# Graph attention on one core: 17 instead of 16 of 52 score pairs weighted by GpSimd, and loads of q and k that write one copy each

## The chip, the core and the metric

The kernel runs on one core of a Trainium2 chip. A core has a matrix engine (TensorE, PE in the profile; its weight loads are PEld), a vector engine (VectorE, DVE), an engine for functions such as the exponential (ScalarE, ACT), an engine of general processors (GpSimd, POOL), and a sequencer that here only issues transfers (SyncE, SP). Each takes its instructions in order and waits for the others by semaphores. Transfers run on 16 DMA engines that all queues share. SBUF is the memory on the chip, PSUM the one that TensorE writes its results into, and DRAM is outside. The metric is device time in microseconds (us); less is better.

## The reference, cut to what matters

```python
def _L1_gnn_ref(x, spatial_encoding, edge_encoding, Wq, Wk, Wv, Wo):
    n, d = x.shape                      # 3327, 128
    h = Wq.shape[0] // d                # 8
    scale = d ** (-0.5)
    q = (x @ Wq.T).reshape(d, n, h)
    k = (x @ Wk.T).reshape(d, n, h)
    v = (x @ Wv.T).reshape(d, n, h)
    a = jnp.einsum('dnh,dmh->dnm', q, k) * scale
    a = a + spatial_encoding + edge_encoding
    a = jax.nn.softmax(a, axis=2)
    out = jnp.einsum('dnm,dmh->dnh', a, v)
    out = out.reshape(n, h * d)
    return out @ Wo.T

# --- layer 0 ---
h = jnp.maximum(_layernorm(x, axis=-1), 0.0)
x = x + _L0_gnn_ref(h, adj, ...)        # one product with adj.T, a batch norm, relu
# --- layer 1 ---
h = jnp.maximum(_layernorm(x, axis=-1), 0.0)
x = x + _L1_gnn_ref(h, adj, adj, ...)
```

All values are fp32. Layer 1 is nearly the whole time. It has 128 batches ("d"), each an attention of 3327 queries over 3327 keys with only 8 numbers per query, and the same 3327 x 3327 matrix, twice adj, is added to the scores of every batch. So the exponentials, 128 x 3327 x 3327 of them, and the sums with the matrix weigh as much as the matrix products.

## The kernel before, in words

**Cutting.** Layer 1 takes the batches in 32 groups of G = 4. Within a group the queries come in 7 blocks (`qblocks`: six of 480, one of 448), the keys in NC = 26 chunks of 128 (key m is in chunk m mod 26). Scores lie with the keys on partitions and the queries along the free dimension. For one chunk and one block, the four batches make two *pairs* (`half` 0 and 1), so a block has 52 pairs. `SU = 13` steps of four pairs make a block; 91 steps make a group; the program is written out flat, with no loop on the chip.

**A pair's way.** `product` makes the scores of both batches into one PSUM tile `s` (two banks, three such tiles). q and k are held as two parts each (a rounded value and its remainder[...]), so each batch takes 32 rows: q's rows are (part 0, part 0, part 1, part 1), 8 rows each, k's rows are (part 0, part 1, part 0, part 1), and their product over 32 rows is the full one. This is why every load of q and k writes its source twice.

There are then two ways. A **plain** pair: VectorE adds the matrix (tile `at`, loaded from `in_adjT`) to the scores and writes `d`; ScalarE later takes the exponential of all plain pairs of the step in one instruction (`late`, L970). A **weighted** pair: ScalarE takes the exponential of the bare scores from PSUM (`f`, L934), and GpSimd multiplies it with the exponential of the matrix (tile `wt`, L937), which was computed once and kept in DRAM as `wd`. Either way `second` multiplies the result with v on TensorE three steps later (`LAG = 3`, L670), into one of two PSUM banks `av`.

**Which pair goes which way.** `kinds` gives every step its pairs. Chunks 0 to WC - 1 are plain, WC = 18 to 25 weighted: 36 and 16 pairs. A step has three plain pairs and one weighted, and the steps in `DOUBLE = (3, 7, 11)` have two and two. So ScalarE's order in a step is f, then the d of the step before; in a double step a second f follows.

**Tiles and loads.** `fetch(x + PRE)` issues on SP what the step two ahead needs first: `at` tiles of two chunks (480 KB, four buffers, 9 a block), `wt` tiles of one chunk (240 KB, three buffers, 8 a block). A load waits on SP until its buffer is free (VectorE's last use for at, GpSimd's for wt), and all that SP issues after it waits too.

**Beside the steps.** During a group, `loads` brings q, k and v of the next one: k in two halves through a staging tile `ks`, sorted by casts on GpSimd (L194), q directly, v in three loads. These items, 33 per group, are spread evenly over steps 4 to 87 (in group 0: over steps 39 to 87, `FROM`). `projections` computes q, k and v of the next but one group in blocks 0 to 2 (k in 0, q in 1, v in 2; in group 0 of two groups): `begin` puts its product into the other av bank in a double step (7 or 11), `go_on` empties it in the same step on VectorE, two more instructions on GpSimd round it (L240, L241), and in the next step (8 or 12) SP stores it (L247 for q and k, L222 for v). In groups 30 and 31 there is none. `outputs` does the last product with Wo in blocks 3 and 4. `finish` divides a finished block of av: three pieces at the steps in `PARTS = (3, 7, 8)`; L702 and L704 store.

**The first group.** `wd` doesn't exist yet. For block 0 `weigh_early` makes it at the end of layer 0; for each later block, `more_weights` does so during the block before: in a cycle of three steps two chunks of the matrix are loaded (L814), two steps later ScalarE takes their exponential (L819), and at the next cycle SP stores them (L806). Before the first step, `first_loads` brings k (all chunks, 4 loads, L879), q of block 0 (8 loads, L883), v (L885); the rest of q (`others`, 8 loads, L915) follows two a step from step 2 on.

The loads of q and k in the code:

```python
qs = qT[:, bass.ds(d * N + n0, n)].rearrange("(a h) n -> a h n", h=H)
...
    q[p0 + a * 2 * H : p0 + (a + 1) * 2 * H, n0 : n0 + n].bitcast(F32),
    qs[a].unsqueeze(0).to_broadcast([2, H, n]),
...
ks = kT[:, bass.ds(d * N + n0, n)]
...
    k[p0 : p0 + 4 * H].bitcast(F32), ks.unsqueeze(0).to_broadcast([2, 2 * H, n])
```

Of the kernel before, what the change touches and what calls it, by code (L numbers as in the profile page):

```python
# [9 lines left out]
F32 = mybir.dt.float32  # L10
# [8 lines left out]
N = 3327  # L19
D = 128  # L20
H = 8
P = 128
NC = 26
T = N * D
NP = NC * P
NB = 512
QB = 480
# [2 lines left out]
HALF = 0.5 / math.sqrt(D)  # L30
SAFE = 30.0
SU = NC // 2
WC = 18
CH = 4 * NP // D
NG = D // G
DOUBLE = (3, 7, 11)
PARTS = (3, 7, 8)

# [6 lines left out]
def tile_two_layer_gnn(  # L47
# [34 lines left out]
    kT = dram.tile([2 * H, TP], F32, name="kT")  # L82
# [6 lines left out]
    wd = dram.tile([NC - WC, P, NP], F32, name="wd")  # L89
# [4 lines left out]
    adjr = adjT.rearrange("(p c) n -> p c n", c=NC)  # L94
# [43 lines left out]
    def q_loads(q, p0, d, n0=0, n=NP):  # L138

        qs = qT[:, bass.ds(d * N + n0, n)].rearrange("(a h) n -> a h n", h=H)  # L140
        return [
            (
                q[p0 + a * 2 * H : p0 + (a + 1) * 2 * H, n0 : n0 + n].bitcast(F32),
                qs[a].unsqueeze(0).to_broadcast([2, H, n]),
            )
            for a in range(2)
        ]

    def k_loads(k, p0, d, n0, n):
        ks = kT[:, bass.ds(d * N + n0, n)]  # L150
        return [(
            k[p0 : p0 + 4 * H].bitcast(F32), ks.unsqueeze(0).to_broadcast([2, 2 * H, n])
        )]

    def v_loads(v, d):
        W = NC * (H + 1)
# [152 lines left out]
    with tc.tile_pool(name="l0", bufs=1) as l0, tc.tile_pool(  # L309
        name="l0adj", bufs=3  # L310
    ) as ap, tc.tile_pool(name="l0s", bufs=4) as sp, tc.tile_pool(
        name="l0last", bufs=1
# [13 lines left out]
        cols = l0.tile([P, 4], F32, name="cols")  # L326
# [162 lines left out]
        for c in range(NC):  # L489
            a = tiles[c]  # L490
# [37 lines left out]
            i = c - 2 * NQ - 5  # L528
# [3 lines left out]
        weights = []  # L532
        for n0 in range(0, NB, NB // 2):
            a = ap.tile([P, 7 * NB], F32, name="a")
            a8 = a[:, : 8 * (NB // 2)].rearrange("p (c n) -> p c n", c=8)
            nc.sync.dma_start(a8, adjr[:, WC:, n0 : n0 + NB // 2])
            weights.append((a8, n0, NB // 2))

# [18 lines left out]
        for i, (n0, w) in enumerate(blocks):  # L557
            s = slice(n0, n0 + w)
# [150 lines left out]
    def attention():  # L709
# [3 lines left out]
        with tc.tile_pool(name="exd", bufs=4) as ep, tc.tile_pool(  # L713
            name="adj", bufs=4
        ) as ap, tc.tile_pool(name="adw", bufs=3) as wp, tc.tile_pool(
            name="exf", bufs=6
        ) as fp, tc.tile_pool(name="res", bufs=2) as rp, tc.tile_pool(
            name="wk", bufs=2
        ) as wk, tc.tile_pool(name="psc", bufs=3, space=PSUM) as psc, tc.tile_pool(
            name="pav", bufs=1, space=PSUM  # L720
# [6 lines left out]
            if True:  # L727
# [14 lines left out]
                for s in range(SU):  # L742
                    j, k = (sum(len(x[i]) for x in kinds) for i in range(2))
                    n = 2 if s in DOUBLE else 1
                    kinds.append((
                        [(x // 2, x % 2) for x in range(j, j + 4 - n)],
                        [(WC + x // 2, 1 - x % 2) for x in range(k, k + n)],
                    ))


                wanted, have = [], {}
                for x, (i, y, s) in enumerate(steps):
                    n0, w = qblocks[y]
# [9 lines left out]
                def fetch(x):  # L763
                    while wanted and wanted[0][0] <= x:
                        _, kind, i, y, c = wanted.pop(0)
                        n0, w = qblocks[y]
                        if kind:
                            a = wp.tile([P, QB], F32, name="wt")
                            nc.sync.dma_start(a[:, :w], wd[c - WC, :, n0 : n0 + w])
                        else:  # L770
                            a = ap.tile([P, 2, QB], F32, name="at")
                            n = min(2, WC - 2 * c)
                            nc.sync.dma_start(
                                a[:, :n, :w], adjr[:, 2 * c : 2 * c + n, n0 : n0 + w]
                            )
                        have[kind, i, y, c] = a
# [20 lines left out]

                def more_weights(i, y, s):

                    k, phase = divmod(s, 3)  # L800
                    if i or y + 1 >= len(qblocks):
                        return
                    n0, w = qblocks[y + 1]
                    c = WC + 2 * k
                    if phase == 0 and k:
                        nc.sync.dma_start(  # L806
                            wd[c - 2 - WC : c - WC, :, n0 : n0 + w].rearrange("c p n -> p c n"),
                            have["w"][:, :, :w],
                        )
                    if c == NC:  # L810
                        return
                    if phase == 0:
                        have["w"] = wk.tile([P, 2, QB], F32, name="t4")
                        nc.sync.dma_start(  # L814
                            have["w"][:, :, :w], adjr[:, c : c + 2, n0 : n0 + w]
                        )
                    elif phase == 2:
                        a = have["w"][:, :, :w]
                        nc.scalar.activation(a, a, AF.Exp, bias=low, scale=2.0)  # L819
# [3 lines left out]
                extra, begun = [], []  # L823

                def begin(i, y, s):
                    if extra and s in DOUBLE[1:]:
                        begun.append(extra.pop(0))
                        drive(begun[0], avs2[(i * len(qblocks) + y + 1) % 2])

# [72 lines left out]
                for x, (i, y, s) in enumerate(steps):  # L902
                    n0, w = qblocks[y]
                    fetch(x + PRE)
                    k = x - i * SU * len(qblocks) - FROM[i]
                    if k == 0 and i + 1 < NG:
                        pending = loads(sets[(i + 1) % 2], at(i + 1))
                        total = len(pending)

                    while pending and (total - len(pending)) * (SU * len(qblocks) - FROM[i] - 4) <= k * total:  # L910
                        pending.pop(0)()
                    more_weights(i, y, s)
                    if x > 1:
                        for args in others[:2]:
                            nc.sync.dma_start(*args)  # L915
                        del others[:2]
                    due = len(waiting) == LAG
                    plain, rest = pairs(s)
                    d = ep.tile([P, 3, 2, QB], F32, name="d")
                    es = [d[:, j] for j in range(len(plain))]  # L920

                    def add(j, p):
                        c = plain[j][0]

                        nc.vector.scalar_tensor_tensor(  # L925
                            d[:, j, :, :w],
                            have[0, i, y, c // 2][:, c % 2, :w]
                            .unsqueeze(1).to_broadcast([P, 2, w]),
                            SAFE / 2, p[:, :, :w], ALU.min, ALU.add,
                        )  # L930

                    def weighted(c, p):
                        f = fp.tile([P, 2, QB], F32, name="f")
                        nc.scalar.activation(  # L934
                            f[:, :, :w], p[:, :, :w], AF.Exp, scale=2.0
                        )
                        nc.gpsimd.tensor_tensor(  # L937
                            f[:, :, :w], f[:, :, :w],
                            have[1, i, y, c][:, :w].unsqueeze(1).to_broadcast([P, 2, w]),
                            ALU.mult,  # L940
                        )
                        es.append(f)

                    if coming is None:
                        coming = first(x)
                    weighted(rest[0][0], coming)
                    coming = None
                    if late is not None:
                        late()
                    add(0, product(i, y, *plain[0]))  # L950
                    second(0)
                    if s == DOUBLE[1]:
                        step()
                    add(1, product(i, y, *plain[1]))
                    if len(rest) > 1:
                        weighted(rest[1][0], product(i, y, *rest[1]))
                    else:
                        add(2, product(i, y, *plain[2]))
                    if s in PARTS and s != DOUBLE[1]:
                        step()  # L960

                    if s - 1 in DOUBLE and x + 1 < len(steps):
                        coming = first(x + 1)
                    second(1)
                    begin(i, y, s)
                    go_on(i, y, s)

                    def late(d=d, w=w, n=len(plain)):
                        flat = d[:, :n].rearrange("p j x n -> p (j x) n")[:, :, :w]
                        nc.scalar.activation(flat, flat, AF.Exp, scale=2.0)  # L970

                    waiting.append(((i, y, s), es))
# [207 lines left out]
```

## Time and profile before

| | |
|---|---|
| time, median of 3 runs | 10234.54 us (10231.9 to 10239.35) |
| the profiled execution | 10253.06 us, its span 10251.3 us |
| granted clock of TensorE, mean | 0.981 |
| TensorE busy | 95% of the span |
| VectorE busy | 91% |
| ScalarE busy | 96% |
| GpSimd busy | 82% |
| DMA | 1735.75 MB, mean 169 GB/s |
| loads of q for a next group (L172) | 248, 208 KB each |
| loads of ks for a next group (L172) | 248, 208 KB each |
| products with the weights on GpSimd (L937) | 3584, mean 2233 ns |

The profile is of one execution. A group of instructions is written as line, engine, operation, output<-inputs with partitions x elements, count, then busy time in us and the mean in ns of one, then the idle time of the engine just before them and what ended most of it. A timeline row is the start, the time taken, engine, line, operation, and in brackets the idle time before it with what ended it; x2 behind a row merges two neighbours. A row of waits is who waited for whom, us in total, times, the longest. "SPq" is SyncE's queue. A matmul's end is modelled, so a busy TensorE isn't TensorE at its peak.

### The profile page before, as it was taken

Reading aid. Unit: us, or ns where it says so; the run is one execution under the profiler, and the core shown is the slowest. Engines: PE = TensorE matmul, PEld = TensorE weight load, DVE = VectorE, ACT = ScalarE, POOL = GpSimd, SP = SyncE. Lnnn points to the kernel's source line nnn. Section 1 sums busy time; section 2 is a strip of 40 time slices with the busy share of each in tenths; the row PEclk is TensorE's granted clock in tenths of the full one; section 3 lists DMA queues with packets and bytes.
Section 4 is the critical chain, followed back from the end, with each engine's and each line's share of the span. In section 5 each row is a group of like instructions: output and inputs, shape, how many; then the busy total and the mean of one; then the engine's idle time right before and its main releaser. Section 6 shows DMA issues by size and latency. Waiting matters only on the chain.

```text
span 10251.3 us, 186610 instructions
## 1 busy us (share of the span) xinstructions
PE 9787.2 (95%) x71535; PEld 2720.9 (27%) x71535; DVE 9306.6 (91%) x9527; ACT 9886.6 (96%) x6662; POOL 8434.3 (82%) x4325
## 2 busy tenths in 40 slices
PE   7899999999999999999999999999999999999998
PEld 3122222222222222222222222222222222222222
DVE  5689999999999999999999999999999999999998
ACT  4799999999999999999999999999999999999998
POOL 1678888888888888888888888888888888888887
PEclk8899999999999999999999999999999999999999
DMA  6665666655666555666556665555666555656554
GB/s 238 195 188 162 169 173 169 170 164 164 169 173 170 168 165 165 170 171 168 168 161 167 168 174 168 164 168 163 170 169 170 167 163 168 171 167 170 162 158 129
DMA packets 1035806, 1735.75 MB, mean 169 GB/s; under 512 B 116086, under 2 KB 1011828, under 8 KB 1027092
## 3 DMA queue, kind: packets, MB, share of 16 engines
q1 hardware_dynamic: 1032399, 1718.85, 59.4%
q8 instruction: 561, 9.19, 0.4%
q0 software_dynamic: 784, 4.03, 0.1%
q14 instruction: 346, 2.83, 0.1%
q10 hardware_dynamic: 1716, 0.85, 0.0%
HBM read 1621.03 MB, written 102.37 MB: 168 GB/s over the span
## 4 chain that ended last, share of the span: by engine, by line
POOL 30%; PE 25%; ACT 20%; issue 11%; DMA 11%; DVE 2%; SPq 1%; POOLq 0%; ACTq 0%; DVEq 0%
POOL f L937 29%; PE av L670 13%; ACT f L934 11%; PE s L785 9%; ACT d L970 9%; DMA at<-in_adjT 6%; DMA wt<-wd 2%; DVE d L925 2%; PE acc L502 1%; DMA t<-in_adjT 1%; PE av L210 1%; POOL k L194 1%; DMA q<-qT 1%; POOL o L241 1%; POOL o L240 0%
## 5 line engine op out<-in xcount | busy, mean ns | idle before, releaser
L925 DVE SCALAR_TENSOR_TENSOR d<-at,s 128x960 f32<-128x960 f32 x8064 | 8733.3, 1138 | 632.9 <-PE s L785 361.2
L937 POOL TENSOR_TENSOR f<-f,wt 128x960 f32<-128x960 f32 (+1 forms) x3584 | 7933.3, 2233 | 1552.2 <-ACT f L934 1322.0
L970 ACT ACTIVATE d<-d 128x2880 f32<-128x2880 f32 (+1 forms) x2912 | 7071.3, 2428 | 97.0 <-DVE d L925 95.8
L670 PE MATMUL av<-d,v 128*9 128x480 f32 x32256 | 5126.0, 573 | 0.6 <-ACT d L970 0.6
L785 PE MATMUL s<-q,k 32*128 32x480 f32 x23296 | 4267.6, 479 | 412.8 <-ACT f L934 179.9
L934 ACT ACTIVATE f<-s 128x960 f32<-128x960 f32 (+1 forms) x3584 | 3443.7, 987 | 54.7 <-PE s L785 48.4
L785 PEld LDWEIGHTS s<-q,k 32*128 32x128 f32 x23296 | 1801.2, 183 | 5745.0 <-DVE d L925 3710.2
L670 PE MATMUL av<-f,v 128*9 128x480 f32 x14336 | 2876.7, 570 | 0.0
L670 PEld LDWEIGHTS av<-d,v 128*9 128x9 f32 x32256 | 585.1, 88 | 1228.0 <-issue 1226.1
L670 PEld LDWEIGHTS av<-f,v 128*9 128x9 f32 x14336 | 317.8, 88 | 154.0 <-issue 139.3
L194 POOL CAST k<-ks 128x256 fp32r<-128x256 f32 x434 | 284.2, 655 | 0.0
L241 POOL TENSOR_TENSOR o<-pf,o 104x512 fp32r<-104x512 f32 x124 | 159.5, 1287 | 9.9
L502 PE MATMUL acc<-a,A 128*128 128x512 f32 (+1 forms) x364 | 152.1, 570 | 9.2 <-DMA a<-in_adj 9.1
L680 DVE STREAM_TRANSPOSE avs<-av 128x480 f32<-128x480 f32 (+1 forms) x224 | 149.5, 667 | 4.4 <-PE av L670 4.4
L512 DVE TENSOR_REDUCE amax<-a 128x1 f32<-128x3327 f32 x26 | 93.7, 3604 | 27.8 <-DMA a<-in_adj 27.8
L444 POOL TENSOR_SCALAR o<-ident,rdeg 128x128 f32<-128x128 f32 x26 | 15.2, 601 | 110.1 <-DVE rdeg L441 110.1
L502 PEld LDWEIGHTS acc<-a,A 128*128 128x128 f32 x364 | 68.9, 192 | 94.9 <-issue 93.4
L509 ACT ACTIVATE junk<-a 128x3327 bf16<-128x3327 f32 x26 | 77.3, 2974 | 6.5 <-DMA a<-in_adj 6.5
L239 DVE TENSOR_SCALAR pf<-av,low_half 104x512 f32<-104x512 f32 x62 | 46.5, 751 | 40.0 <-PE av L210 38.8
L237 DVE COPY pf<-av 104x512 f32<-104x512 f32 x62 | 42.8, 691 | 39.5 <-PE av L210 39.5
L819 ACT ACTIVATE t<-t,low_half 128x960 f32<-128x960 f32 (+1 forms) x24 | 26.2, 1090 | 52.2 <-DMA t<-in_adjT 49.2
L240 POOL CAST o<-pf 104x512 fp32r<-104x512 f32 x124 | 76.1, 613 | 0.0
(131 smaller groups left out, 916.7 us busy)
## 6 DMA issues: line engine op xcount, KB each, us to landing
at<-in_adjT SPq DMA_DIRECT2D x1728, 480.0 KB
wt<-wd SPq DMA_DIRECT2D x1536, 240.0 KB
at<-in_adjT SPq DMA_DIRECT2D x288, 448.0 KB
wt<-wd SPq DMA_DIRECT2D x256, 224.0 KB
ks<-kT SPq DMA_DIRECT2D x248, 208.0 KB
q<-qT SPq DMA_DIRECT2D x248, 208.0 KB
a<-in_adj SPq DMA_DIRECT2D x26, 1663.5 KB
kT<-o SPq DMA_DIRECT2D x128, 208.0 KB
```

Source lines behind the costliest of these rows:

```text
L194: nc.gpsimd.tensor_copy(k[:, c : c + n, half * 64 : half * 64 + 64], ks.bitcast(F32).rearrange("g (p c) -> g c p", c=NC)[:, c : c + n, :],)
L210: nc.tensor.matmul(bank[:CH], hj, wqk[s][:, e * NB : (e + 1) * NB], start=True, stop=True)
L241: nc.gpsimd.tensor_tensor(o[:CH, 1], f[:CH], of[:CH, 0], ALU.subtract)
L502: nc.tensor.matmul(acc[i][:, :w], A[:, c, :], a[:, n0 : n0 + w], start=(c == 0), stop=(c == NC - 1),)
L512: nc.vector.tensor_reduce(amax[:, c : c + 1], a[:, :N], AX.X, ALU.max, apply_absolute_value=True)
L670: nc.tensor.matmul(av[32 * b : 32 * b + H + 1, :w], tiles[2][:, b, c, :], e, start=first, stop=last,)
L680: nc.vector.transpose(avs[:, :J, :].rearrange("p j h -> p (j h)"), av[:, : 32 * J].rearrange("p (q j) -> p j q", j=J),)
L785: nc.tensor.matmul(p[:, x, :we], k[rs, c, :], q[rs, n0 : n0 + we], start=True, stop=True,)
L925: nc.vector.scalar_tensor_tensor(d[:, j, :, :w], have[0, i, y, c // 2][:, c % 2, :w] .unsqueeze(1).to_broadcast([P, 2, w]), SAFE / 2, p[:, ...
L934: nc.scalar.activation(f[:, :, :w], p[:, :, :w], AF.Exp, scale=2.0)
L937: nc.gpsimd.tensor_tensor(f[:, :, :w], f[:, :, :w], have[1, i, y, c][:, :w].unsqueeze(1).to_broadcast([P, 2, w]), ALU.mult,)
L970: nc.scalar.activation(flat, flat, AF.Exp, scale=2.0)
```

## The change

Five things change together.

- One pair more goes the weighted way: 35 plain pairs (`PP`), 17 weighted. Chunk 17 (`WC` is now 17) has its half 0 plain and its half 1 weighted, so it is loaded both as part of an `at` tile and as a `wt` tile (9 a block), and `wd` has nine chunks.
- Four double steps instead of three: 2, 5, 8 and 11. A block has 9 steps of 3 + 1 and 4 of 2 + 2.
- What hangs on those steps moves: the pieces of `finish` to steps 5, 8 and 9, the begin of a side product to 8 and 11 (its store to 9 and 12). The weighted pairs take their halves in the order 0, 1 instead of 1, 0.
- `more_weights` takes three chunks in a cycle of four steps instead of two in three (loads at steps 0, 4, 8, exponentials at 2, 6, 10, stores at 4, 8, 12); `weigh_early` nine chunks instead of eight.
- Each load of q and k writes one copy: for q four loads of 8 rows per batch instead of two with a broadcast source, for k two of 16 rows instead of one. A group's k and q take 32 loads instead of 16, its list 49 items instead of 33; `first_loads` has 8 and 16 of them instead of 4 and 8, `others` 16 instead of 8. The bytes are the same.

```diff
-WC = 18
+PP = 35
+WC = PP // 2
 CH = 4 * NP // D
 NG = D // G
-DOUBLE = (3, 7, 11)
-PARTS = (3, 7, 8)
+DOUBLE = (2, 5, 8, 11)
+PARTS = (5, 8, 9)
...
         qs = qT[:, bass.ds(d * N + n0, n)].rearrange("(a h) n -> a h n", h=H)
         return [
-            (
-                q[p0 + a * 2 * H : p0 + (a + 1) * 2 * H, n0 : n0 + n].bitcast(F32),
-                qs[a].unsqueeze(0).to_broadcast([2, H, n]),
-            )
-            for a in range(2)
+            (q[p0 + i * H : p0 + (i + 1) * H, n0 : n0 + n].bitcast(F32), qs[i // 2])
+            for i in range(4)
         ]
 
     def k_loads(k, p0, d, n0, n):
-        ks = kT[:, bass.ds(d * N + n0, n)]
-        return [(
-            k[p0 : p0 + 4 * H].bitcast(F32), ks.unsqueeze(0).to_broadcast([2, 2 * H, n])
-        )]
+        cols = bass.ds(d * N + n0, n)
+        return [
+            (k[p0 + i * 2 * H : p0 + (i + 1) * 2 * H].bitcast(F32), kT[:, cols])
+            for i in range(2)
+        ]
...
-            a8 = a[:, : 8 * (NB // 2)].rearrange("p (c n) -> p c n", c=8)
+            a8 = a[:, : (NC - WC) * (NB // 2)].rearrange("p (c n) -> p c n", c=NC - WC)
...
-                        [(WC + x // 2, 1 - x % 2) for x in range(k, k + n)],
+                        [((PP + x) // 2, (PP + x) % 2) for x in range(k, k + n)],
...
-                            n = min(2, WC - 2 * c)
+                            n = min(2, (PP + 1) // 2 - 2 * c)
...
-                    k, phase = divmod(s, 3)
+                    k, phase = divmod(s, 4)
...
-                    c = WC + 2 * k
+                    c = WC + 3 * k
                     if phase == 0 and k:
                         nc.sync.dma_start(
-                            wd[c - 2 - WC : c - WC, :, n0 : n0 + w].rearrange("c p n -> p c n"),
+                            wd[c - 3 - WC : c - WC, :, n0 : n0 + w].rearrange("c p n -> p c n"),
...
-                        have["w"] = wk.tile([P, 2, QB], F32, name="t4")
+                        have["w"] = wk.tile([P, 3, QB], F32, name="t4")
                         nc.sync.dma_start(
-                            have["w"][:, :, :w], adjr[:, c : c + 2, n0 : n0 + w]
+                            have["w"][:, :, :w], adjr[:, c : c + 3, n0 : n0 + w]
...
-                    if extra and s in DOUBLE[1:]:
+                    if extra and s in DOUBLE[2:]:
...
-                    if s == DOUBLE[1]:
+                    if s == DOUBLE[2]:
                         step()
...
-                    if s in PARTS and s != DOUBLE[1]:
+                    if s in PARTS and s != DOUBLE[2]:
                         step()
```

## The prediction

> **What bounds the kernel now.** I read the page's engine shares and costliest groups first, to see which engine has the least room.
>
> ```profile
> PE 9787.2 (95%) x71535; PEld 2720.9 (27%) x71535; DVE 9306.6 (91%) x9527; ACT 9886.6 (96%) x6662; POOL 8434.3 (82%) x4325
> ...
> L925 DVE SCALAR_TENSOR_TENSOR d<-at,s 128x960 f32<-128x960 f32 x8064 | 8733.3, 1138 | 632.9 <-PE s L785 361.2
> L937 POOL TENSOR_TENSOR f<-f,wt 128x960 f32<-128x960 f32 (+1 forms) x3584 | 7933.3, 2233 | 1552.2 <-ACT f L934 1322.0
> L970 ACT ACTIVATE d<-d 128x2880 f32<-128x2880 f32 (+1 forms) x2912 | 7071.3, 2428 | 97.0 <-DVE d L925 95.8
> L934 ACT ACTIVATE f<-s 128x960 f32<-128x960 f32 (+1 forms) x3584 | 3443.7, 987 | 54.7 <-PE s L785 48.4
> ```
>
> Three engines are above 90%, so shares alone decide nothing. The chain of waits is no better here: it gives POOL 30%, PE 25% and ACT 20%. So next the windows view, cut at the first exponential (L934) of a group: rows are the first group, group 15, and group 30, counted from 0. Columns: window, length, busy of PE, PEld, DVE, ACT, POOL, clock, DMA share, GB/s.
>
> ```profile
> 266.14:663.37 397.23, 336.41 (x2159) 83.04 (x2158) 289.65 (x288) 327.70 (x226) 268.49 (x142) 0.86 0.64 196
> 4981.17:5288.93 307.76, 298.20 (x2222) 81.68 (x2220) 286.03 (x291) 304.24 (x204) 262.98 (x135) 0.99 0.60 168
> 9614.60:9918.25 303.65, 292.30 (x2210) 81.80 (x2210) 283.22 (x285) 303.65 (x205) 256.06 (x127) 1.00 0.59 163
> ```
>
> In group 30 ScalarE is busy 303.65 of 303.65 us: it is the bound. The timeline of ScalarE gives its real price, the spacing of starts, since neighbours overlap:
>
> ```profile
> 5064.60 0.96 ACT L934 ACTIVATE f<-s 128x960 f32<-128x960 f32 x1
> 5065.44 2.60 ACT L970 ACTIVATE d<-d 128x2880 f32<-128x2880 f32 x1
> 5067.94 1.83 ACT L934 ACTIVATE f<-s 128x960 f32<-128x960 f32 x2
> 5069.64 1.82 ACT L970 ACTIVATE d<-d 128x1920 f32<-128x1920 f32 x1
> 5071.33 0.99 ACT L934 ACTIVATE f<-s 128x960 f32<-128x960 f32 x1
> ```
>
> f costs 0.85, a d of three pairs 2.50, a d of two 1.70 us. Medians of all spacings are 0.850, 2.496 and 1.694, so a block of 480 queries needs 16 x 0.850 + 10 x 2.496 + 3 x 1.694 = 43.64 us; blocks in the trace take 43.6 to 43.8 wherever nothing stalls. Group starts follow from the same rows: group 0 takes 397.2, groups 1 to 29 308.7 on average, group 30 303.6. So the time above the ScalarE floor is 29 x 5.0 = 145 us in groups 1 to 29, 94 us in group 0, and the start ahead of 266 us.
>
> The 5 us sit in blocks 1 and 2 of a group. The timeline of SyncE and VectorE in group 15:
>
> ```profile
> 5018.14 0.65 SPq L172 DMA_DIRECT2D ks<-kT  x1
> 5024.98 1.69 SPq L247 DMA_DIRECT2D kT<-o  x2
> 5026.77 0.41 SPq L773 DMA_DIRECT2D at<-in_adjT  x1
> ...
> 5029.79 1.53 SPq L172 DMA_DIRECT2D v<-v  x1
> ...
> 5036.01 3.28 DVE L925 SCALAR_TENSOR_TENSOR d<-at,s 128x960 f32<-128x960 f32 x3 [2.00 <-DMA at<-in_adjT]
> ```
>
> SP holds 6.2 us for the projection's cast on POOL; the next at tile is issued at 5026.77 and lands only at 5036, 9 us for 480 KB. Its packets show why: loads of ks leave a backlog. Their 6656 B packets take 0.253 us, run only two at a time, and those of the last ks load run from 5026 to 5031. Group 30 has the same loads but no projection, and no stall: it takes hold and backlog together.
>
> At the start the same width is plainer: the DMA view of 217 to 257 us in 40 slices, then SP, then two rows of the waits.
>
> ```profile
> DMA  3011111169899999511111111111111111111111
> GB/s 91 27 53 61 53 53 53 53 283 455 342 423 432 426 437 416 238 61 55 55 47 55 55 53 53 53 53 53 53 67 53 53 53 53 53 53 53 53 53 53
> ```
> ```profile
> 214.51 2.90 SPq L879 DMA_DIRECT2D k<-kT  x4
> 217.53 41.53 SPq L883 DMA_DIRECT2D q<-qT  x8
> ```
> ```profile
> ACT t L819 <- DMA t<-in_adjT: 49.2, 11, 19.7
> PE s L785 <- DMA q<-qT: 39.6, 2, 38.5
> ```
>
> A flat 53 GB/s at about 0.12 of 16 engines (the hump is the store of hd and xd) is two engines at 26 GB/s. TensorE waits 38.5 us for it.
>
> **What the Trainium skill says.** DMA: Bandwidth & Descriptors, section "Why a DMA increments its semaphore by 16 and not by 1": a DMA is spread over the largest k up to 16 that divides the slowest dimension of both access patterns. A leading broadcast of 2 gives k = 2, which the 53 GB/s confirms; 16 rows give 16, 8 rows 8. ScalarE: Activation LUTs, section "What ACT_TABLE_LOAD costs": 186 ns + 0.833 N, neighbours overlapping by 93 ns; for N = 2880 that is 2.492, the trace has 2.496. GPSIMD Engine Reference, section 3.1: about 2.6 cycles an element, by estimate 960 x 2.6 / 1.2 GHz = 2.08 us plus dispatch; the trace spaces products by 8.87 / 4 = 2.22 us.
>
> **The change, part by part.**
> 1. First loads. k: 8 issues at 0.725 (2.90 / 4) = 5.8 us; q: 16 at the shortest issue seen, 0.61 = 9.8. The last q is issued at 214.5 + 15.6 = 230.1 instead of 259.1, and the data of k is then never what is late: its 128 packets of 0.5 us are 4 us on 16 engines. Everything behind (v, at, t) moves with it: -29. Bounds -20 (the stores of hd and xd, 3.3 MB, now collide) to -34.
> 2. Group 0. The 19.7 us wait for t stands behind the "others", 8 loads of q on two engines (2 x 26 GB/s for 1.4 MB is 27 us); on eight engines it goes: -20. The other 29.5 us of waits for t come mostly in blocks 3 to 5, beside the k and q loads; I take 12 of them off, and give 4 back for t loads of 720 instead of 480 KB, still awaited two steps after their issue (ScalarE at steps 2, 6, 10 instead of 2, 5, 8, 11; f and d queue behind them): -28 together. Bounds 0 and -60.
> 3. Stalls of groups 1 to 29. Loads of k stop overfilling two engines (208 KB at 53 GB/s are 4.0 us, one every 2.5 steps or 8.4 us, so 48% on top of a DMA share near 0.6), v moves from steps 2, 4, 7 of block 1 to 5, 7, 8 (49 items paced over 83 steps instead of 33), away from the burst after the hold, and the first double step comes at 2 instead of 3. The hold itself stays (store at step 12). I keep a fifth of 145: -115. Bounds 0 and -145.
> 4. ScalarE, on the path: a d of three becomes one of two plus one f: 0.850 + 1.694 - 2.496 = +0.048, x 224 blocks = +11. In group 0, three exponentials of 1440 instead of four of 960 per block (spacing 0.98; estimate 1.38): +1. weigh_early, 2 x 256 elements and 12% more DMA: +1.
> 5. VectorE loses 224 sums, 245 us at 1.093 spacing, hidden: it isn't the bound. It makes recovery after a late tile quicker, counted in 3.
> 6. GpSimd gains 224 products, 497 us: a block is 17 x 2.22 = 37.7, casts of k about 1.4, and in blocks 0 and 1 two projections of 1.9: 41.5 of 43.7. Hidden, by 2 us. Products are used three steps (10 us) later, so a backlog of 2 us after steps 8 and 11 drains unseen.
> 7. SP: 16 more issues a group, some 10 us, under its 4306 us of waits for POOL f at L769; nothing while these exist. 224 more wt tiles are 54 MB on 1736, 3%.
> 8. With nine wt tiles in three buffers, five of them replace a tile that was last used one step before instead of two. SP then stands about one step later there, and at, stores and loads queue behind it. The next at is still issued three steps ahead by the order of the program: 0.
> 9. finish and projections move with DOUBLE and PARTS (steps 5, 8, 9; begins at 8, 11): same work, begun in steps where VectorE has two sums; the 14 casts of k stay, in blocks 2, 3, 5 and 6 on POOL: 0.
>
> Sum: -29 - 28 - 115 + 13 = -159. Against the profiled execution (10253.1, span 10251.3) that is 10094; the median shown is 18.5 lower, so 10075.
>
> **Rivals.**
> - All stalls go: group 30 as the pattern, -29 - 60 - 145 + 13 = -221, 10013. For: no stall there at all. Against: the hold stays and POOL's cast comes later.
> - The hold alone causes the stalls: only the start and the first t wait are won, -29 - 22 + 13, 10197. For: group 30 lacks the hold. Against: the 9 us landing, and the second half of k, in blocks 4 and 5 without a hold, stalls nothing either, so a backlog alone is harmless, a hold alone untested.
> - Slower: point 8 bites. SP stands behind wt until POOL's product is done, at lands late, VectorE and so ScalarE stall in every block. Five such loads a block, 224 blocks: 0.16 us at each eats 179 us, the gain and 0.2% more; at 1 us a block 10299. For: SP's longest wait in total is already L769 on POOL f. Against: three steps are 10 us, an at tile lands in some 3 us when nothing is jammed.
> - The loads aren't spread: two engines still, nothing at the start, some 10240.
>
> **How the numbers follow.** The forecast 64% (10040 to 10115), all stalls gone 14%, hold alone 12%, slower 6%, not spread 4%. About 0.2% (20 us) is what can be told from no change. Faster 0.90, same 0.04, slower 0.06. Range 10005 to 10165: the first two and the near part of the third.
>
> **What would show it.** First f near 237 instead of 266; no plateau of 53 GB/s; the t wait of 19.7 gone; blocks 1 and 2 of a group within 1 us of 43.7; a quiet block 0.05 longer; POOL near 87%. Wrong if VectorE's waits for at exceed 137 us, if POOL's products delay av beyond the 14 us now seen, or if blocks 3 to 6 take over 44 us.

## The result, and the profile after

| | before | after |
|---|---|---|
| time, median | 10236.94 us (4 runs, 10231.9 to 10239.62) | 10130.65 us (4 runs, 10127.19 to 10139.72) |
| ratio, 95% interval | | 0.9898, 0.9881 to 0.9915 |
| the profiled execution | 10253.06, span 10251.3 | 10139.72, span 10137.9 |
| first f of ScalarE (start of the attention) | 266.1 | 240.9 |
| group 0, from its first f to the next group's | 397.2 | 380.6 |
| groups 1 to 29, mean | 308.66 | 306.18 |
| group 30 | 303.65 | 304.39 |

The change is faster by 1.0%, 106 us; the forecast was 159. The difference of the two profiled spans, 113.4 us, divides by the first starts of f as the forecast did: start 25.2, group 0 16.6, groups 1 to 29 29 x 2.48 = 71.9; groups 30 and 31 and the tail gave back 0.6 in all. (Times of groups and blocks, here and below, are taken from the starts of f in the one profiled execution of each kernel.)

The page after, engine shares and the groups that answer to those shown before:

```profile
PE 9726.2 (96%) x71535; PEld 2720.2 (27%) x71535; DVE 9142.1 (90%) x9303; ACT 9904.7 (98%) x6880; POOL 8916.1 (88%) x4549
...
L936 POOL TENSOR_TENSOR f<-f,wt 128x960 f32<-128x960 f32 x3808 | 8419.4, 2234 | 984.6 <-ACT f L933 944.3
L924 DVE SCALAR_TENSOR_TENSOR d<-at,s 128x960 f32<-128x960 f32 x7840 | 8566.0, 1141 | 734.5 <-PE s L784 379.1
L969 ACT ACTIVATE d<-d 128x2880 f32<-128x2880 f32 (+1 forms) x2912 | 6896.3, 2368 | 17.2 <-DVE d L924 15.2
...
L933 ACT ACTIVATE f<-s 128x960 f32<-128x960 f32 x3808 | 3639.0, 988 | 75.3 <-PE s L784 65.5
```

GpSimd and VectorE moved as counted: 224 products more, 224 sums fewer. ScalarE's idle time ahead of d fell from 97.0 to 17.2 us, and its share rose to 98%. The windows view again, groups 0, 14 and 30 (columns as before: window, length, PE, PEld, DVE, ACT, POOL, clock, DMA share, GB/s):

```profile
240.94:621.53 380.59, 337.81 (x2156) 84.31 (x2156) 282.22 (x280) 330.67 (x228) 284.91 (x149) 0.86 0.74 217
4597.64:4912.33 314.69, 303.04 (x2225) 82.14 (x2228) 281.57 (x284) 305.05 (x211) 278.05 (x142) 0.97 0.63 170
9500.68:9805.07 304.39, 292.36 (x2210) 81.51 (x2210) 277.89 (x278) 304.35 (x212) 271.06 (x134) 1.00 0.61 168
```

Group 30 is still ScalarE and nothing else, at 0.74 us more than before. Group 14 is the worst of the others: 314.69, with ScalarE idle for some 10 us. So stalls are rarer, not gone. The DMA view of 217 to 257 us shows what the loads changed at the start:

```profile
GB/s 335 414 122 200 186 186 186 186 120 212 163 301 407 418 418 458 438 427 376 248 244 254 153 261 323 398 394 398 230 283 23 0 0 0 0 148 301 34 149 399
```

Nothing is left of the plateau at 53 GB/s. In block 1 of group 14, where it stalls, SyncE, GpSimd and VectorE stand like this:

```profile
4643.34 1.72 SPq L246 DMA_DIRECT2D kT<-o  x2
4646.91 0.35 SPq L768 DMA_DIRECT2D wt<-wd  x1
...
4647.84 0.91 SPq L772 DMA_DIRECT2D at<-in_adjT  x2
```
```profile
4643.39 1.29 POOL L240 TENSOR_TENSOR o<-pf,o 104x512 fp32r<-104x512 f32 x1
4644.63 13.24 POOL L936 TENSOR_TENSOR f<-f,wt 128x960 f32<-128x960 f32 x6
```
```profile
4654.38 3.28 DVE L924 SCALAR_TENSOR_TENSOR d<-at,s 128x960 f32<-128x960 f32 x3 [2.72 <-DMA at<-in_adjT]
```

After the projection's rounding, GpSimd works off six products, 13.24 us without a gap. SP stores the projection, then stands before a wt load until the first of those products has given its buffer back (4646.91). A load of ks and two of at stand behind it; the first at tile lands 6.4 us after its issue, at 4654.26, and is 2.7 us late for VectorE. That is step 8 of the forecast, which was priced at nothing.

### The profile page after: what moved, and what is told of

Its sections match the earlier page's. It is cut to its first block, busy times and chain, and to the rows that moved or that the text cites. A ratio compares the mean times of both kernels' runs of the same rounds, so it can differ in the third digit from the quotient of the medians.

```text
span 10137.9 us, 188102 instructions
## 1 busy us (share of the span) xinstructions
PE 9726.2 (96%) x71535; PEld 2720.2 (27%) x71535; DVE 9142.1 (90%) x9303; ACT 9904.7 (98%) x6880; POOL 8916.1 (88%) x4549
## 5 line engine op out<-in xcount | busy, mean ns | idle before, releaser
L936 POOL TENSOR_TENSOR f<-f,wt 128x960 f32<-128x960 f32 x3808 | 8419.4, 2234 | 984.6 <-ACT f L933 944.3
L924 DVE SCALAR_TENSOR_TENSOR d<-at,s 128x960 f32<-128x960 f32 x7840 | 8566.0, 1141 | 734.5 <-PE s L784 379.1
L969 ACT ACTIVATE d<-d 128x2880 f32<-128x2880 f32 (+1 forms) x2912 | 6896.3, 2368 | 17.2 <-DVE d L924 15.2
L669 PE MATMUL av<-d,v 128*9 128x480 f32 x31360 | 4871.1, 569 | 0.6 <-ACT d L969 0.6
L784 PE MATMUL s<-q,k 32*128 32x480 f32 x23296 | 4224.1, 478 | 361.9 <-ACT f L933 237.3
L933 ACT ACTIVATE f<-s 128x960 f32<-128x960 f32 x3808 | 3639.0, 988 | 75.3 <-PE s L784 65.5
L669 PEld LDWEIGHTS av<-d,v 128*9 128x9 f32 x31360 | 560.2, 88 | 1155.3 <-issue 1153.7
L286 PEld LDWEIGHTS av<-wo,t 128*104 128x104 f32 x512 | 60.0, 173 | 50.4 <-DVE oq L690 25.2
```

The costliest lines, as they stand in the source:

```text
L669: nc.tensor.matmul(av[32 * b : 32 * b + H + 1, :w], tiles[2][:, b, c, :], e, start=first, stop=last,)
L784: nc.tensor.matmul(p[:, x, :we], k[rs, c, :], q[rs, n0 : n0 + we], start=True, stop=True,)
L924: nc.vector.scalar_tensor_tensor(d[:, j, :, :w], have[0, i, y, c // 2][:, c % 2, :w] .unsqueeze(1).to_broadcast([P, 2, w]), SAFE / 2, p[:, ...
L933: nc.scalar.activation(f[:, :, :w], p[:, :, :w], AF.Exp, scale=2.0)
L936: nc.gpsimd.tensor_tensor(f[:, :, :w], f[:, :, :w], have[1, i, y, c][:, :w].unsqueeze(1).to_broadcast([P, 2, w]), ALU.mult,)
```

## The experiments

The theory: loads on two engines leave a backlog that turns SP's hold (its wait before a store for the projection's rounding) into a stall, so the loads won the time. The rival: the double steps, by relieving VectorE, removed the stalls, and the loads count at the start alone. The first four kernels ran on one chip beside the kernel before (10229.41, nine runs), the other four on another chip (10260.24, nine runs); each ratio is to the kernel before on the same chip.

**The loads alone.** The kernel before with `q_loads` and `k_loads` of the change, nothing else:

```diff
-                qs[a].unsqueeze(0).to_broadcast([2, H, n]),
...
+            (q[p0 + i * H : p0 + (i + 1) * H, n0 : n0 + n].bitcast(F32), qs[i // 2])
+            for i in range(4)
...
-            k[p0 : p0 + 4 * H].bitcast(F32), ks.unsqueeze(0).to_broadcast([2, 2 * H, n])
...
+            (k[p0 + i * 2 * H : p0 + (i + 1) * 2 * H].bitcast(F32), kT[:, cols])
+            for i in range(2)
```

> The kernel before with only the loads of q and k changed to one copy each; 16 weighted pairs, three double steps as before. Theory (two-engine loads leave a backlog that turns SP's hold into a stall): start about 25 us earlier, group 0 about 17 shorter, groups 1 to 29 lose most of their 5.0 us of stalls and keep the lower ScalarE floor of 303.65: mean 304.5 to 305.5, time 10070 to 10095. Rival (the double steps, by relieving VectorE, removed the stalls; the loads matter at the start alone): groups stay at 308.7, time about 10195.

Measured: 10066.7 us, ratio 0.984 (0.9826 to 0.9853). First f at 238.1, group 0 371.3, groups 1 to 29 304.04, group 30 303.75. All of the theory's numbers, each a little better than its range. The waits show that SP's hold is as long as ever (first line; 511.4 us in the kernel before), ScalarE's wait for t fell from 49.2 to 13.0 us (second), and the page gives ScalarE's d almost no idle time (third):

```profile
SPq L245 <- POOL o L238: 561.0, 124, 6.7
```
```profile
ACT t L817 <- DMA t<-in_adjT: 13.0, 7, 3.0
```
```profile
L968 ACT ACTIVATE d<-d 128x2880 f32<-128x2880 f32 (+1 forms) x2912 | 7075.8, 2430 | 4.5 <-DVE d L923 2.4
```

So a hold without a backlog stalls almost nothing: 0.3 us a group is left. That the burst of transfers behind a hold asks too much of all 16 engines is no rival: in the 10 us after the last store of k in groups 1 to 29 the DMA share is 0.97 in the kernel before and 0.99 here. One thing moves along with the width: the longer list puts the loads of v at steps 5, 7 and 8 of block 1 instead of 2, 4 and 7, and no run keeps them in place. It can't be the whole: 50 of the 118 us that VectorE waited for at in groups 1 to 29 lay in blocks 2 and 3, where no v is loaded, and those went too.

The narrow loads also stop SP itself. In the kernel before, SP waits for loads of ks and q to land, 130 us in all from group 1 on; here 0.5 us are left, and in the changed kernel none. The largest row before:

```profile
SPq L773 <- DMA ks<-kT: 75.1, 57, 3.1
```

No run divides the two ways in which a narrow load delays at, on the engines and on SP. And this half of the change is faster than the whole: the weighting costs 64 us by the medians (10130.65 - 10066.7), some 59 by the two ratios to the kernel before (0.9898 against 0.984, whose intervals lie apart).

**The weighting alone.** The changed kernel with the old loads of q and k:

```diff
 WC = PP // 2
 DOUBLE = (2, 5, 8, 11)
...
-            (q[p0 + i * H : p0 + (i + 1) * H, n0 : n0 + n].bitcast(F32), qs[i // 2])
...
+                qs[a].unsqueeze(0).to_broadcast([2, H, n]),
...
```

> The changed kernel with the old loads of q and k, two copies each by a broadcast source; 17 weighted pairs and four double steps stay. Theory: first exponential back at 266, backlog back, stalls of 5 us a group or more on top of the higher ScalarE floor of 304.4: mean of groups 1 to 29 309 to 311, time 10250 to 10300. Rival (double steps removed the stalls): groups at 306, time about 10175.

Measured: 10553.53 us, ratio 1.0314 (1.03 to 1.0328), worse than either theory said. Groups 1 to 29 318.95; and group 30, which has no projection, takes 313.9. Most of its excess sits in blocks 1 and 5, 48.0 and 47.7 us, in which or just before which k is loaded. SP, then VectorE, in block 5 of group 13 (it is no single case: 106.6 us of VectorE's waits for at lie in block 5 of groups 1 to 29):

```profile
4724.06 0.35 SPq L770 DMA_DIRECT2D wt<-wd  x1
4724.46 0.66 SPq L173 DMA_DIRECT2D ks<-kT  x1
4725.17 0.92 SPq L774 DMA_DIRECT2D at<-in_adjT  x2
...
4726.66 0.66 SPq L173 DMA_DIRECT2D ks<-kT  x1
4731.95 0.34 SPq L770 DMA_DIRECT2D wt<-wd  x1
```
```profile
4734.97 3.28 DVE L926 SCALAR_TENSOR_TENSOR d<-at,s 128x960 f32<-128x960 f32 x3 [3.80 <-DMA at<-in_adjT]
```

The at loads of 4725.17 arrive only at 4735. SP issues in bursts, because it stands before wt, and loads of ks in the same burst fill two engines. The waits of VectorE for at, in the kernel before, after and here:

```profile
DVE d L925 <- DMA at<-in_adjT: 136.7, 98, 11.3
DVE d L924 <- DMA at<-in_adjT: 48.5, 48, 2.7
DVE d L926 <- DMA at<-in_adjT: 327.7, 156, 7.1
```

SP itself also stood before at for loads of q that had not landed, which the changed kernel does not:

```profile
SPq L774 <- DMA q<-qT: 176.8, 63, 4.9
```

Here a backlog needs no projection to stall: that the wt loads are hold enough is the reading, which the fifth kernel below puts to the test.

**No hold, the backlog kept.** The kernel before, with the stores of the k and q projections issued by GpSimd:

```diff
-                        extra.extend(projections(wk, hj, j, False, ov, low_half[:CH, 1:2]))
+                        extra.extend(projections(
+                            wk, hj, j, False, ov, low_half[:CH, 1:2],
+                            (nc.gpsimd, nc.gpsimd, nc.sync),
+                        ))
```

> The kernel before, but the stores of the q and k projections in the attention are issued from GpSimd's queue instead of SP's, so SP is not held by them; the loads keep their broadcast. Theory (it takes the hold and the backlog together): stalls of groups 1 to 29 fall to 1 us or less, as in group 30, mean 304.0 to 305.0, start and group 0 nearly as before, time 10100 to 10125. Rival A (the backlog of two engines alone): 308.7 stays, time about 10237. Rival B (VectorE has no room): the same 10237.

Measured: 10101.37 us, ratio 0.9872 (0.9857 to 0.9887). Groups 1 to 29 303.76, against 303.66 in its group 30: the stalls are gone though the loads still use two engines. GpSimd's busy time rises by 186.4 us for the 248 stores, 0.75 us each. VectorE's waits for at, of which 17.1 us now lie in group 0:

```profile
DVE d L928 <- DMA at<-in_adjT: 31.3, 18, 11.2
```

With this, both halves of the stall of the kernel before are shown: it takes hold and backlog together, and either remedy is enough.

**A fourth wt buffer.** The changed kernel with four, and y sharing the tile of xj to make room:

```diff
-        ) as ap, tc.tile_pool(name="adw", bufs=3) as wp, tc.tile_pool(
+        ) as ap, tc.tile_pool(name="adw", bufs=4) as wp, tc.tile_pool(
...
-        y = wk.tile([P, D], F32, name="y")
+        y = xj
```

> The changed kernel with four wt buffers instead of three (the output tile y shares the tile xj to make room, in the once-a-group outputs). Theory for what is left (1.8 us of stalls in groups 1 to 29: SP stands behind a wt load while GpSimd works off the projections, and at tiles come late): mean of groups 306.2 falls to 304.6 to 305.2, VectorE's waits for at fall from 48 us to under 20, time 10085 to 10105. Rival (what is left is VectorE's own work after a projection): no change, 10131.

Measured: 10110.59 us, ratio 0.9879 (0.9864 to 0.9894; the changed kernel's 0.9881 to 0.9915 overlaps, so the step between the two rests on the group times and the waits). Groups 305.39: of the 1.8 us that were left, 0.8 went. VectorE's waits for at are 15.9 us instead of 48.5, and SP's wait before wt halves (the changed kernel first, then four buffers):

```profile
SPq L768 <- POOL f L936: 6330.3, 1940, 8.6
```
```profile
SPq L768 <- POOL f L936: 3166.2, 1368, 5.8
```

The group time missed its range by a little (304.6 to 305.2), and the time too (10085 to 10105). So the tight wt loads are not quite half of what was left.

**The weighting with broadcast loads and four buffers.** The second kernel above with the same two edits.

> The run with the weighting edit and the old broadcast loads (10553), with four wt buffers instead of three (y shares xj). Theory: its 14 us of stalls a group, also where no projection is (group 30: 313.9), come from SP standing behind wt loads that replace a tile used one step before, on top of the two-engine backlog; a fourth buffer puts the distance back to two steps or more, and what is left is about the 5 us of the kernel before: groups 1 to 29 309 to 311, time 10260 to 10320. Rival (GpSimd's extra product, or the DMA bytes, cause them): 10550 stays.

Measured: 10331.29 us, ratio 1.007 (1.0053 to 1.0088), a little above the range. The second kernel was 324 us slower than the kernel before, this one is 71 us slower; the two profiled spans differ by 228. Group 30 falls from 313.9 to 304.66, groups 1 to 29 from 318.95 to 311.58, VectorE's waits for at from 327.7 to 163.6 us. GpSimd's products and the bytes are the same in both, so for this larger part it is the distance between a wt load and the last use of its buffer that the weighting spoiled. What is left needs the projections, as before the change: nearly all of it is in block 1, which takes 50.6 us (50.3 with three buffers, 47.3 in the kernel before), and group 30 is free of it.

**The changed kernel with four buffers and the stores on GpSimd.**

> The changed kernel with four wt buffers and with the stores of the q and k projections on GpSimd's queue. Theory: both of what holds SP is gone, groups 1 to 29 fall from 305.4 (four buffers alone) to 304.3 to 304.7, the ScalarE floor of 17 weighted pairs; time 10075 to 10090. Rival (what is left is GpSimd's own lateness with 17 products; the stores on its queue add to it): 305.4 or more, 10110 and up.

Measured: 10098.61 us, ratio 0.9845 (0.9832 to 0.9859). Groups 304.97, between the theory (304.3 to 304.7) and the rival (305.4), and so is the time. With both remedies, 17 weighted pairs still take about 1 us a group more than 16 in the next kernel; 0.9 of it stands in group 30 too (304.69 against 303.81), so most of it needs no projection.

**The loads with the stores on GpSimd.** The first kernel with the edit of the third:

> The kernel before with one-copy loads and the stores of the q and k projections on GpSimd's queue. Theory: the 0.3 us left per group goes too, groups at 303.7; time 10050 to 10065, the fastest. Rival (nothing is left to win at the stores, and their issue on GpSimd costs): 10067 or more.

Measured: 10056.84 us, ratio 0.9806 (0.9792 to 0.9819), the fastest kernel of this study. Groups are at 303.94 (303.7 was expected), 0.1 less than with the loads alone; group 0 takes 363.4 instead of 371.3, while its start is 5 us later. The two kernels ran on different chips, where the kernel before itself differed by 0.3%, so the step from 10066.7 is not settled. Against the kernels before and after of the comparison the gain is clear.

**Fifteen weighted pairs.** The kernel just told, one pair further the other way:

```diff
-WC = 18
-DOUBLE = (3, 7, 11)
-PARTS = (3, 7, 8)
+PP = 37
+WC = PP // 2
+DOUBLE = (4, 10)
+PARTS = (4, 10, 11)
...
-                    if extra and s in DOUBLE[1:]:
+                    if extra and s in DOUBLE:
```

> The same with 15 weighted pairs instead of 16 and two double steps (4 and 10), one step the other way on the same scale. Theory (each weighted pair costs ScalarE 0.05 to 0.1 us a block): floor 0.3 to 0.7 us a group lower, if VectorE keeps up with 37 sums (37 x 1.093 = 40.4 of 43.6 us a block before its other work): groups 303.0 to 303.4, time 10035 to 10050. Rival (VectorE becomes the bound): groups above 306, time above 10120.

Measured: 10119.39 us, ratio 0.9865 (0.9849 to 0.9881). Groups 305.67: neither theory's numbers, near the rival's, and slower than 16. In blocks 3 and 5 the floor did fall, to 43.73 and 43.71 from 43.79 and 43.78; but blocks 0 to 2, where VectorE also empties the projections, take 44.1 to 44.3, and so does block 4. In group 30, which has no projection, blocks 0 to 2 take 43.6 to 43.7, so in those it is the projections that cost. The page:

```profile
PE 9782.3 (97%) x71535; PEld 2768.5 (27%) x71535; DVE 9465.6 (94%) x9751; ACT 9891.3 (98%) x6438; POOL 8158.2 (81%) x4349
```

VectorE is at 94%. That it is VectorE that sets those blocks, having no room for side work beside its sums, is argued from this row and the count of sums, not shown. The trace speaks against it as the whole reason: in block 3 VectorE has 1.2 us of work for the output and the block stays at 43.73, in block 4 it has 0.6 and the block takes 44.3.

## Why the prediction was right, and where it was off

The forecast of 10075 missed by 56 us inside its range; the direction and the bound held. It was no luck of errors that cancel: each of the four terms of the sum won less or cost more than was forecast. Point by point, by the profiled executions:

1. **First loads**: -29, measured -25.2. The plateau is gone as foretold. The last q was issued at 234.5, not 230.1: not the issue (0.27 us for 8 rows) but waits of SP for earlier loads to land set the pace, 6.8 us for loads of k and 2.3 for q.
2. **Group 0**: -28, measured -16.6. With the loads alone it was -25.9, so the step was right for the loads; the weighting gave 9.3 back. The DMA share is 0.74 in both; the cause stays open.
3. **Stalls**: -115, measured -93: stalls of 5.0 us a group became 306.18 - 304.39 = 1.8. With the loads alone they became 0.3, worth -137. The mechanism, backlog and hold together, was right, as the first and third experiments show; what the forecast kept for caution, a fifth, was too much for the loads and too little for the whole.
4. **ScalarE's order**: +11, measured 0.74 a group or +24. The sum of spacings, 0.048 a block, is right as far as it goes; a quiet block took 0.09 more than before, and block 6 of group 30 0.23. The difference is not divided: small waits, such as 0.1 us before d at step 10, come to about as much in the kernel before, at steps 9 and 10.
5. **VectorE and GpSimd** (5 and 6): VectorE's lost sums were hidden, and GpSimd's products came in time for TensorE, whose waits for them before av fell from 14.2 to 7.0 us. But that GpSimd's backlog after a projection "drains unseen" was wrong: av didn't see it, SP did, before wt.
6. **SP's issues** (7): some 2 us a group instead of 10. A load of ks takes 0.42 us to issue and one of q 0.33, where each of the half as many before took 0.64.
7. **The wt distance** (8) is the step that failed. It was priced at 0, because at is issued three steps ahead "by the order of the program". That order is worth what SP's progress is worth: wherever GpSimd was behind, SP stood before wt and the three steps shrank. The row below is the kernel before; the change made it 6330.3 us. The sum alone proves little, since SP only changes the place where it stands: with the fourth buffer its wait before at rose from 123.7 to 1960.8, and the fastest kernel, the loads with the stores on GpSimd, has 5281.8 before wt. What shows the cost is the fourth buffer.

```profile
SPq L769 <- POOL f L937: 4306.6, 1513, 5.8
```

With the old loads that buffer took back 228 us by the profiled spans. With spread loads the weighting adds 29 x 1.5 = 44 us of stalls (306.18 - 304.39 against 0.3); the fourth buffer took back 29 x 0.8 = 23 of them, and the rest is not assigned. The rival that ended slower had this mechanism; it deserved a price in the forecast's own sum. What the forecast held against that rival, that an at tile lands in some 3 us, was the best case: over the kernel before, the time from issue to landing is 3.3 us at the least, 5.2 at the median and over 10 for one load in ten; after, the median is 5.3 and one in ten takes over 6.6.

The rival "the hold alone" fell with the first experiment; "not spread" fell with the DMA view. Said in advance and found: first f near 237 (240.9), the t wait of 19.7 gone (the longest is 2.3), blocks 1 and 2 within 1 us of 43.7 (44.5 and 44.6), POOL near 87% (88%). None of the signs of being wrong showed: VectorE's waits for at are 48.5 us, those for av 7.0, and blocks 3 to 6 stay under 44.

So of the change, the loads won some 163 us and the weighting lost some 60. Measured by their own runs, the parts don't add: the weighting costs 324 us on the old loads and a fifth of that on the new. "The weighting" is here all of the change but the loads: no run divides the seventeenth pair from the double steps and what moved with them.

## What to carry to other kernels

A transfer that is narrow on the DMA engines can harm those that queue behind it, and not only itself: look in the packets for a flat rate, and for loads that take 9 us to land where the same load elsewhere takes 3 to 5. When a change makes a tile's buffer be replaced sooner after its last use, price the wait on the issuing queue and everything behind it, however far ahead the program seems to issue; a spare buffer, or another queue for the one store that holds it, was a cheap remedy here. And run each half of a double change: here the smaller-looking half carried all the gain, and the other took a third of it away.

## What the runs showed of the hardware that was not expected

The split loads were issued in less time than the ones they replaced: 0.27 to 0.33 us for 8 rows and 0.42 for 16, against 0.64 with the broadcast source. The number of rows alone doesn't explain it: the broadcast load of q writes 16 rows and took 0.64, as did that of ks with 32, while a load of k with 16 rows and no broadcast took 0.42.

On SP, this program's loads take turns on eight completion semaphores, so a ninth waits for the first to land: at the start after the change, eight of the loads of q waited for loads of k, some 0.85 us each. This is also why SP stood still for narrow loads within the groups: 130 us from group 1 on in the kernel before, 255 with the weighting on the old loads, 0 after.
